# Last layer on quarters of TensorE: column product, mean and loads of x rearranged

## The chip, the cores and the metric

The program runs on one core of one Trainium2 chip. The metric is device time in microseconds (us), the median of three runs.

## The reference

Two layers on one image of 48 channels, 256 x 256, in fp32. Layer 0 is an attention over patches (group norm, a 1x1 product to q, k and v, a 3x3 depthwise convolution, attention in eight heads, a projection, the residual); the change doesn't touch it. Layer 1, cut to what matters:

```
def _L1_conv_ref(x, Ws, Hs, Cs, window_size):
    B, C, H, W = x.shape
    ws = window_size
    xb = x.reshape(B, C, H // ws, ws, W // ws, ws)
    out = jnp.einsum('bcphqw,twW,thH,tcC->bCpHqW', xb, Ws, Hs, Cs)
    return out.reshape(B, C, H, W)
...
x = x + _L1_conv_ref(_gn(x), L1_conv_Ws, L1_conv_Hs, L1_conv_Cs, 64)
```

`_gn` is a group norm with 16 groups of 3 channels. In each 64 x 64 window, and for each of three terms t, x is multiplied over its channels by Cs (48 x 48), over its columns by Ws (64 x 64) and over its rows by Hs (64 x 64); the three terms are added up.

## The kernel before, in words

The first 3230 us or so are layer 0's attention; the scheduler of the tile framework places the instructions there, and those of the next stage that are ready early slip in at its end.

**Projection and statistics (L765 to L835).** In eight steps of 16 rows from each half of the image, SyncE loads the attention's output and the input x, TensorE projects (L790), VectorE adds the residual (L797) and takes the statistics of the sum (L801), and GpSimd's queue stores the sum to a DRAM tensor `x1s` (L806). After the last step `group_stats` (L127 to L146) makes mean and reciprocal deviation: a chain of small products and VectorE instructions, with products `pm` (L132) and `pv` (L139). Then `csn`, the matrix Cs with its rows scaled by the reciprocal deviation (L828), and `cbias`, the mean times csn on all 128 partitions (L832, L834).

**Last layer (L838 to L954).** A unit is a row of windows (64 image rows, index yw) times half the width (128 columns, two windows, index xh): eight units. Each has three products:

- `over_c` (L863), the channel product: for each pair of image rows, a product of 48 channels by 128 columns with csn (144 wide: three terms by 48). The upper and lower 32 rows of the unit lie on partitions 0 to 47 and 64 to 111 of `lxq`, so two products run on two row halves of TensorE. VectorE evicts three row pairs at a time to `lzt` and subtracts cbias there (L881), eleven evictions a unit.
- `over_w` (L889), the column product: `lzt` has the 128 columns on its partitions and is the stationary operand, 64 wide; `wsb` (128 x 128 per term) is the moving one: Ws twice on the diagonal, zeros elsewhere. The two products for two groups of channels go to two column halves of TensorE. ScalarE copies each tile `pb` (128 x 512, two PSUM buffers) to `lyt` (L903).
- `over_h` (L906), the row product: `hsb` (64 x 64) stationary, `lyt` moving, 64 x 64 on each quarter of TensorE, 512 columns, three terms added up in PSUM. `residual` (L922) adds x from `lrt` on VectorE (L925), and GpSimd's queue stores to the output (L928).

The order of this stage is written out by hand (`manual_schedule`, L935): the channel product of unit 0 first; then, for every unit, three rounds (q) of eight channels from each half: two column products of four channels each from both halves (three tiles `pb` each), after each of them two groups of the next unit's channel product, and then the row product of the round before. x is loaded twice from SyncE's queue, both in packets of 512 B (128 columns): `lxq` two units ahead with the channels on the partitions (L762), `lrt` at a unit's start with image rows on the partitions (L857).

In TensorE's counts each fp32 product stands as two instructions.

Of the kernel before, what the change touches and what calls it, by code (L numbers as in the profile page):

```python
# [16 lines left out]
C = 48  # L17
# [3 lines left out]
KS = 4  # L21
# [24 lines left out]
def conv_preact_kernel(  # L46
# [80 lines left out]
    def group_stats(st, mean, rstd, pool, pspool):  # L127
# [4 lines left out]
        nc.tensor.matmul(pm, lhsT=gm, rhs=mv[:, 0:1], start=True, stop=True)  # L132
        nc.vector.tensor_copy(mean, pm)
# [5 lines left out]
        nc.tensor.matmul(pv, lhsT=gm, rhs=e, start=True, stop=True)  # L139
        f = pool.tile([P2, 1], F32, name="gsf")  # L140
# [609 lines left out]
    lx = ctx.enter_context(tc.tile_pool(name="lx", bufs=3))  # L750
    HW = WS // 2
    units = [(yw, xh) for yw in range(H // WS) for xh in range(2)]
    xqs = {}

    def load_x(u):

        yw, xh = units[u]
        xcol = slice(xh * 128, (xh + 1) * 128)
        xq = lx.tile([64 + C, HW, 128], F32, name="lxq")
        for s in range(2):  # L760
            y0 = yw * WS + s * HW
            nc.sync.dma_start(out=xq[s * 64 : s * 64 + C], in_=x1s[:, y0 : y0 + HW, xcol])  # L762
        xqs[u] = xq

    with tc.tile_pool(name="pj", bufs=3) as pj, tc.tile_pool(name="pjs", bufs=1) as pjs, tc.tile_pool(  # L765
# [41 lines left out]
        for u in range(2):  # L807
            load_x(u)

        gm2 = pjs.tile([P2, 64 + C], F32, name="gm2")  # L810
        nc.vector.memset(gm2, 0.0)
        for o in (0, 64):
            nc.vector.tensor_copy(gm2[:, o : o + C], gm[:, 0:C])
        mv1, e1 = group_stats(st1, mean1, rstd1, pjs, pp1)
        pc1 = pp1.tile([64 + C, 1], F32, name="pc1", tag="pstat")
        nc.tensor.matmul(pc1, lhsT=gm2, rhs=e1, start=True, stop=True)
        rstd2 = l1c.tile([64 + C, 1], F32, name="rstd2")
        nc.vector.tensor_scalar_add(rstd2, pc1, EPS)
        nc.scalar.activation(rstd2, rstd2, AF.Sqrt)
        nc.vector.reciprocal(rstd2, rstd2)  # L820

        csn = l1c.tile([64 + C, T3 * C], F32, name="csn")
        for s in range(2):
            nc.scalar.dma_start(
                out=csn[s * 64 : s * 64 + C].rearrange("c (t d) -> c t d", t=T3), in_=Cs.rearrange("t c d -> c t d")
            )
            r = slice(s * 64, s * 64 + C)
            nc.vector.tensor_scalar_mul(csn[r], csn[r], rstd2[r])  # L828
        mrow = pjs.tile([C, 128], F32, name="mrow")
        nc.vector.tensor_scalar_mul(mrow, ones, mean1[0:C])  # L830
        pb1 = pp1.tile([128, T3 * C], F32, name="pb1")
        nc.tensor.matmul(pb1, lhsT=mrow, rhs=csn[0:C], start=True, stop=True)  # L832
        cbias = l1c.tile([128, T3 * C], F32, name="cbias")
        nc.vector.tensor_copy(cbias, pb1)  # L834
# [3 lines left out]
    with tc.tile_pool(name="lz", bufs=2) as lz, tc.tile_pool(name="lr", bufs=2) as lr, tc.tile_pool(name="ly", bufs=4) as ly, tc.tile_pool(name="ps1", bufs=2, space=PSUM) as ps1, tc.tile_pool(  # L838
        name="ps2", bufs=2, space=PSUM
    ) as ps2, tc.tile_pool(name="ps3", bufs=1, space=PSUM) as ps3:  # L840
        wsb = lz.tile([128, T3, 128], F32, name="wsb", bufs=1)
        nc.vector.memset(wsb, 0.0)
        hsb = lz.tile([128, T3, WS], F32, name="hsb", bufs=1)
        for s in range(2):
            r = slice(s * WS, (s + 1) * WS)
            nc.scalar.dma_start(out=wsb[r, :, r], in_=Ws.rearrange("t w v -> w t v"))
            nc.scalar.dma_start(out=hsb[r], in_=Hs.rearrange("t h g -> h t g"))
        NQ = 3
        rts, zts, parts = {}, {}, {}

        def load_rows(u):

            yw, xh = units[u]
            xcol = slice(xh * 128, (xh + 1) * 128)
            rt = lr.tile([128, NQ * 8, 128], F32, name="lrt")
            for s in range(2):
                nc.sync.dma_start(  # L857
                    out=rt[s * WS : (s + 1) * WS],
                    in_=x1s[s * 24 : (s + 1) * 24, yw * WS : (yw + 1) * WS, xcol].rearrange("c y x -> y c x"),
                )  # L860
            rts[u] = rt

        def over_c(u):  # L863

            xq = xqs[u]
            zt = zts[u] = lz.tile([128, T3 * C, WS], F32, name="lzt")
            zv = zt.rearrange("p k (s y) -> p s y k", s=2)
            for y0 in range(0, HW, 3):
                n = min(3, HW - y0)
                pa = ps1.tile([128, 2, 512], F32, name="pa")  # L870
                for i in range(n):
                    for s in range(2):
                        r = slice(s * 64, s * 64 + C)
                        nc.tensor.matmul(  # L874
                            pa[:, s, i * T3 * C : (i + 1) * T3 * C],
                            lhsT=xq[r, y0 + i, :],
                            rhs=csn[r],
# [3 lines left out]
                nc.vector.tensor_tensor(  # L881
                    zv[:, :, y0 : y0 + n, :],
                    pa[:, :, : n * T3 * C].rearrange("p s (y k) -> p s y k", y=n),
                    cbias.rearrange("p (u v k) -> p u v k", u=1, v=1).to_broadcast([128, 2, n, T3 * C]),
                    ALU.subtract,
                )
                yield

        def over_w(u, c0, c1):  # L889

# [105 lines left out]
```

## Time and profile before

| what | value |
|---|---|
| median of three runs | 3678.31 us (3673.84 to 3683.65) |
| span of the profiled execution | 3669.5 us |
| TensorE busy in the span | 3466.2 us (94%) |
| VectorE, ScalarE, GpSimd busy | 2139.8, 1873.5, 542.7 us |
| first channel product starts | 3370.2 us |
| first column product starts | 3390.6 us |
| last row product ends | 3661.5 us |
| column product L896, instructions | 2304 |
| channel product L874, instructions | 1024 |
| row product L913, instructions | 576 |

The profile is of one execution. Its page gives the busy time of each engine, a map of 40 slices, the chain of work that ended last (followed back from the end, at each step to what released it), and groups of equal instructions: line, engine, operation, output and inputs, shape, count, busy time in us and mean of one in ns, then the idle time of the engine just before them and what ended it. PE is TensorE's product, PEld its load of the stationary operand, DVE VectorE, ACT ScalarE, POOL GpSimd, SP SyncE; a q after it means its queue. In lists in order of time the first two numbers are start and duration in us.

### The profile page before, as it was taken

The page shows a single profiled execution, that of the slowest core. Times are in us where ns is not written, and L with a number is a line of the kernel's source. Part 1 is how long each engine was busy: PE and PEld are TensorE (multiplying, and loading weights), DVE is VectorE, ACT ScalarE, POOL GpSimd, SP SyncE. Part 2 cuts the span into 40 slices and gives each one's busy share as a digit, 9 for nine tenths or more (in the row PEclk, how much of TensorE's full clock was granted, in tenths as well). Part 3 has the DMA queues.
Part 4 walks back from the last instruction along what each step waited for, and adds up shares of the span by engine and source line. Part 5 has one row for each costly group of instructions (what it writes and reads, how often), then busy time and mean ns, then how long its engine had stood idle before and what let it go on. Part 6 is the DMA issues. An engine that isn't in the chain of part 4 may idle for free.

```text
span 3669.5 us, 100344 instructions
## 1 busy us (share of the span) xinstructions
PE 3466.2 (94%) x44252; PEld 2907.3 (79%) x44252; DVE 2139.8 (58%) x3518; ACT 1873.5 (51%) x2747; POOL 542.7 (15%) x630
## 2 busy tenths in 40 slices
PE   2869999999999999999999999999999999965998
PEld 1337788889988888889899988888899888833776
DVE  5464674179628952895389439934993222267654
ACT  0235676566646654665466556655664444400332
POOL 2030211012211211121112112211221100010011
PEclk9989999999999999999999999999999999976999
DMA  7455665533322332333233323332333220089674
GB/s 161 154 131 147 180 171 168 158 97 92 94 72 82 98 90 80 83 93 87 78 82 92 94 76 87 86 93 71 94 84 87 65 53 19 15 213 240 116 136 93
DMA packets 275427, 386.49 MB, mean 105 GB/s; under 512 B 77330, under 2 KB 211842, under 8 KB 270952
## 3 DMA queue, kind: packets, MB, share of 16 engines
q1 hardware_dynamic: 235942, 264.95, 27.3%
q0 software_dynamic: 35552, 106.40, 12.6%
q10 hardware_dynamic: 3490, 8.64, 1.1%
q8 instruction: 350, 5.73, 0.7%
q14 instruction: 93, 0.76, 0.1%
HBM read 234.76 MB, written 144.90 MB: 103 GB/s over the span
## 4 chain that ended last, share of the span: by engine, by line
PE 84%; DVE 3%; issue 2%; DMA 2%; ACT 1%; SPq 0%; POOL 0%; ACTq 0%; POOLq 0%; DVEq 0%
PE big L337 37%; PE big L601 36%; PE pb L896 4%; PE pa L874 2%; PE pc L913 2%; DVE acc L228 1%; PE big L177 1%; PE pt L618 1%; PE pn L247 1%; DMA pot<-os__70 1%; PE pst L555 1%; DMA x1s<-pxt 0%; DMA kt<-qkv 0%; DMA t<-ot 0%; DVE ss L243 0%
## 5 line engine op out<-in xcount | busy, mean ns | idle before, releaser
L572 ACT ACTIVATE e<-big,nmx 128x1024 f32<-128x1024 f32 x1024 | 1143.9, 1117 | 878.4 <-PE big L337 617.5
L337 PE MATMUL big<-kt,qt 128*128 128x512 f32 x6144 | 1437.5, 393 | 30.2 <-DMA kt<-qkv 29.3
L601 PEld LDWEIGHTS big<-vn,e 128*64 128x64 f32 x32768 | 1358.6, 137 | 57.8 <-ACT e L572 30.6
L601 PE MATMUL big<-vn,e 128*64 128x96 f32 x32768 | 1388.9, 247 | 6.5 <-DVE oacc L612 3.0
L337 PEld LDWEIGHTS big<-kt,qt 128*128 128x128 f32 x6144 | 1146.3, 188 | 277.3 <-issue 29.2
L612 DVE TENSOR_TENSOR oacc<-big,oacc 128x768 f32<-128x768 f32 x480 | 453.5, 954 | 713.4 <-PE big L601 713.4
L228 DVE SCALAR_TENSOR_TENSOR acc<-pad,dwt,acc 126x1024 f32<-126x1024 f32 x592 | 765.6, 1293 | 39.5 <-ACT acc L209 23.7
L295 POOL DMA_DIRECT2D qkv<-o x72 | 52.7, 732 | 1242.2 <-ACT o L279 1242.2
L585 DVE TENSOR_REDUCE zt<-zs 128x1 f32<-128x4 f32 x256 | 38.5, 150 | 335.7 <-ACT e L572 335.7
L289 POOL TENSOR_TENSOR ol<-o,oh 126x1024 fp32r<-126x1024 f32 x78 | 184.6, 2367 | 311.6 <-DVE ss L243 238.9
L572 ACT ACTIVATION_READ_ACCUMULATOR e<-big,nmx 128x1 f32 x1024 | 196.4, 192 | 0.0
L903 ACT COPY lyt<-pb 128x512 f32<-128x512 f32 x144 | 84.3, 586 | 201.6 <-PE pb L896 201.6
L881 DVE TENSOR_TENSOR lzt<-pa,cbias 128x864 f32<-128x864 f32 (+1 forms) x88 | 137.0, 1628 | 85.3 <-PE pa L874 85.3
L279 ACT COPY o<-acc 126x1024 f32<-126x1024 f32 x74 | 158.6, 2143 | 0.0
L896 PEld LDWEIGHTS pb<-wsb,lzt 128*64 128x64 f32 x2304 | 125.9, 138 | 29.4 <-issue 19.7
L896 PE MATMUL pb<-wsb,lzt 128*64 128x128 f32 x2304 | 141.9, 279 | 2.8 <-issue 1.6
L623 POOL DMA_DIRECT2D os__70<-oo x128 | 64.9, 513 | 534.4 <-ACT oo L621 533.8
L790 PE MATMUL pps<-pot,wp 96*96 96x512 f32 x128 | 78.0, 777 | 55.2 <-DMA pot<-os__70 44.3
L239 ACT ACTIVATE sq<-acc 126x1024 f32<-126x1024 f32 x74 | 78.2, 1057 | 101.6 <-DVE acc L228 101.6
L180 ACT ACTIVATE ot<-big,bias 108x1024 f32<-108x1024 f32 x64 | 68.2, 1110 | 111.1 <-PE big L177 62.8
L209 ACT ACTIVATE acc<-pad,dwt 126x1024 f32<-126x1024 f32 x74 | 84.1, 1137 | 79.9 <-DMA pad<-t 79.9
L243 DVE TENSOR_REDUCE ss<-sq 126x64 f32<-126x1024 f32 x80 | 97.5, 1219 | 24.6 <-ACT sq L239 24.6
(127 smaller groups left out, 1904.8 us busy)
## 6 DMA issues: line engine op xcount, KB each, us to landing
pad<-t SPq DMA_DIRECT2D x238, 254.0 KB
t<-ot SPq DMA_DIRECT2D x128, 217.7 KB
qkv<-ol POOLq DMA_DIRECT2D x78, 336.0 KB, 6.4
qkv<-oh POOLq DMA_DIRECT2D x70, 336.0 KB, 5.6
qt<-qkv SPq DMA_DIRECT2D x176, 96.0 KB
xs<-in_x_dram SPq DMA_DIRECT2D x128, 96.0 KB
os__70<-oo POOLq DMA_DIRECT2D x128, 96.0 KB, 2.1
pot<-os__70 SPq DMA_DIRECT2D x16, 768.0 KB
```

What stands on the lines that cost most here:

```text
L209: nc.scalar.mul(self.acc, self.pad[:, 0:KS, 0:W], dwt[:, self.h, 0:1])
L228: nc.vector.scalar_tensor_tensor(self.acc, self.pad[:, dy : dy + KS, dx : dx + W], dwt[:, self.h, tap : tap + 1], self.acc, ALU.mult, ALU.add,
L243: nc.vector.tensor_reduce(self.ss, self.sq.rearrange("p a (x b) -> p x a b", b=KS), AX.XY, ALU.add)
L279: nc.scalar.copy(self.o.rearrange("p (a b) x -> p a b x", a=KS), self.acc.rearrange("p a (x b) -> p a b x", b=KS))
L289: eng.tensor_sub(self.ol, self.o, self.oh.bitcast(F32))
L337: nc.tensor.matmul(ps[:, i, :], lhsT=qt[:, r, q0 : q0 + 128], rhs=kts[2 * j + i][:, r // 2, :], start=(r == 0), stop=(r == 2),)
L572: nc.scalar.activation(e[:, j * 1024 : (j + 1) * 1024], ps.rearrange("p a b -> p (a b)"), AF.Exp, bias=nmx[:, b : b + 1], accum_out=zs[:, ...
L601: nc.tensor.matmul(ps[p : p + 64, j // 4, j % 4 * HD : (j % 4 + 1) * HD], lhsT=e[:, mb * 128 + p : mb * 128 + p + 64], rhs=vn, start=(i == 0),
L612: nc.vector.tensor_add(oaccs[h, k], ps[:, :, : 4 * HD], oaccs[h, k])
L881: nc.vector.tensor_tensor(zv[:, :, y0 : y0 + n, :], pa[:, :, : n * T3 * C].rearrange("p s (y k) -> p s y k", y=n), cbias.rearrange("p (u v ...
L896: nc.tensor.matmul(pb[s * WS : (s + 1) * WS, i, :], lhsT=zts[u][:, t * C + c + i, :], rhs=wsb[:, t, :], start=True, stop=True,)
L903: nc.scalar.copy(yt[:, t, :], pb.rearrange("p i x -> p (i x)"))
```

## The change

Seven parts, all in the last layer and just before it:

1. The column product takes quarters of TensorE. `wsb` holds Ws once per half of the partitions (128 x 3 x 64, no zeros and no memset). A tile `pb2` is now 128 x 2 x 512 for one term t and a whole round: 32 products of 64 rows by 64 columns, where the half of the partitions (w) picks the window and the PSUM bank, and s the group of channels. A round has three such tiles. There is one buffer for them; in the last unit they use the two buffers of `pa`, and VectorE copies the tile of t = 1.
2. The mean becomes a 49th row. The pieces of x are set to 1.0 at the beginning, so that row 48 (and 112) stays 1; row 48 of csn is minus the mean times csn (`mcol`, `pb1`, and a subtraction on VectorE). Evictions of the channel product are plain copies, one in four of them on ScalarE, in unit 0 one in two.
3. x is held by full image rows: five pieces of 8 row pairs of all 256 columns (`pieces`, `lx` with five tiles of 8 KB per partition instead of three of 16 KB). Unit 2n and unit 2n + 1 use the same pieces. The channel product has twelve groups a unit (3, 3 and 2 row pairs for every piece).
4. The loads after the first ones come from ScalarE's queue, one by one between its copies (`begin_load`): a piece in four loads of 48 x 4 rows, the x for the residual (`lrt`, now 8 channels by full rows, six buffers) in four loads of 64 x 4 channels for each round of a row of windows. The first pieces and the first `lrt` stay with SyncE.
5. Stores of the output go out by full rows after the second unit of a row of windows; in the last row of windows after each unit.
6. In the statistics TensorE gets products whose result nobody reads (`occupy`), seven before `pm` and one after each of `pm`, `pv`, `pc1` and `pb1`.
7. Within a round the order is: tile 0, two channel groups, tile 1, two channel groups, tile 2, the row product of the round before.

In the built change the five memsets of the pieces stand on VectorE's queue among the last four accumulations of the attention (two ahead of them, one between each two); the first waits for 18 semaphores.

```
-    def group_stats(st, mean, rstd, pool, pspool):
+    def group_stats(st, mean, rstd, pool, pspool, behind=lambda: None):
...
         nc.tensor.matmul(pm, lhsT=gm, rhs=mv[:, 0:1], start=True, stop=True)
+        behind()
...
+    pieces = [lx.tile([64 + CK, PR, W], F32, name=f"lxq{i}") for i in range(NPC + 1)]
+    for t in pieces:
+        nc.vector.memset(t, 1.0)
...
+    def load_piece(yw, i, s, y, n, eng):
+
+        y0 = yw * WS + s * HW + i * PR + y
+        eng.dma_start(out=piece(yw, i)[s * 64 : s * 64 + C, y : y + n, :], in_=x1s[:, y0 : y0 + n, :])
...
-        for u in range(2):
-            load_x(u)
...
+        for i in range(len(pieces)):
+            for s in range(2):
+                load_piece(*divmod(i, NPC), s, 0, PR, nc.sync)
...
+        busy = pps.tile([P2, KS, 128], F32, name="pps")
+
+        def occupy(n):
+
+            for _ in range(n):
+                nc.tensor.matmul(busy[:, 0:2, :], lhsT=ident[:, :P2], rhs=nmx, start=True, stop=True)
+
+        with tc.manual_schedule(engines={mybir.EngineType.PE}):
+            occupy(7)
+            mv1, e1 = group_stats(st1, mean1, rstd1, pjs, pp1, lambda: occupy(1))
...
+            nc.vector.tensor_scalar_mul(csn, csn, rstd2)
+            mcol = pjs.tile([C, 64 + CK], F32, name="mcol")
+            nc.vector.tensor_scalar_mul(mcol, at, mean1[0:C])
+            pb1 = pp1.tile([64 + CK, T3 * C], F32, name="pb1")
+            nc.tensor.matmul(pb1, lhsT=mcol, rhs=csn[0:C], start=True, stop=True)
+            occupy(1)
+            nc.vector.tensor_sub(csn, csn, pb1)
...
+        def rows_later(yw, q):
+
+            if yw < H // WS:
+                for s in range(2):
+                    for c in (0, 4):
+                        loads.append(lambda s=s, c=c: load_rows(yw, q, s, c, 4, nc.scalar))
...
+        def begin_load():
+
+            if loads:
+                loads.pop(0)()
...
+                    if (p * 3 + g) % (4 if u else 2) == 1:
+                        nc.scalar.copy(to, src)
+                    else:
+                        nc.vector.tensor_copy(to, src)
+                    if xh and g == 2:
+                        piece_later(yw * NPC + p + len(pieces))
+                    yield
...
+        def over_w(u, q, t):
+
+            end = u == NU - 1
+            pb = (ps1 if end else ps2).tile([128, 2, 512], F32, name="pb2", tag="pa" if end else "pb2")
+            for n in range(8):
+                b, i = divmod(n, 4)
+                for s in range(2):
+                    for w in range(2):
+                        r = slice(w * WS, (w + 1) * WS)
                         nc.tensor.matmul(
+                            pb[s * WS : (s + 1) * WS, w, n * WS : (n + 1) * WS],
+                            lhsT=zts[u][r, t * C + b * 24 + q * 8 + s * 4 + i, :],
+                            rhs=wsb[r, t, :],
                             start=True,
                             stop=True,
                         )
+            (nc.vector.tensor_copy if end and t == 1 else nc.scalar.copy)(
+                parts[u, q][:, t, :].rearrange("p (n w x) -> p w n x", w=2, x=WS),
+                pb.rearrange("p w (n x) -> p w n x", x=WS),
+            )
...
+                    for t in range(T3):
+                        over_w(u, q, t)
+                        begin_load()
+                        if t < 2:
+                            for _ in range(2):
+                                next(ahead, None)
+                                begin_load()
+                        elif late:
+                            over_h(*late)
```

## The prediction

> **What bounds the kernel now.** I read, in this order, the 40 slices of the page (where the last layer lies), the chain of work that ended last with its pieces in order of time, the groups by shape, and the busy time by stretch. The change touches only what runs after about 3205 us, so the chain from there on is what counts. First the start of the last layer:
>
> ```profile
> 3369.85 0.61 PE pb L832
> 3370.46 1.71 PE pa L874 x11
> 3372.19 1.64 DVE lzt L881
> 3373.88 1.83 PE pa L874 x12
> 3375.73 1.65 DVE lzt L881
> ...
> 3386.39 4.20 DVE lzt L881 x3
> 3390.63 4.75 PE pb L896 x48
> ```
>
> Until 3390.63 only the channel product of unit 0 runs. Two groups of rows take 3.55 us (3373.88 to 3377.43): TensorE is at half clock, and VectorE needs 1.65 us for each eviction, so both are late by turns. The clock is in the busy time by stretch (after PE, PEld, DVE, ACT and POOL stand the granted clock and the DMA share):
>
> ```profile
> 3370.00:3390.60 20.60, 18.09 (x130) 15.92 (x130) 17.48 (x14) 0.00 (x0) 0.00 (x0) 0.50 1.12 165
> 3395.00:3630.00 235.00, 233.41 (x3332) 179.03 (x3332) 142.69 (x96) 72.62 (x124) 26.42 (x38) 1.00 0.67 123
> ```
>
> In the second stretch TensorE is busy 233 of 235 us at full clock, VectorE 61%, ScalarE 31%. It is TensorE's own order of work that sets the end; one round (a third of a unit) and the last one, without a channel product, look like this in the chain:
>
> ```profile
> 3425.96 2.86 PE pb L896 x48
> 3428.82 1.67 PE pa L874 x24
> 3430.49 2.86 PE pb L896 x48
> 3433.35 1.67 PE pa L874 x24
> 3435.02 2.73 PE pc L913 x24
> ...
> 3649.00 5.57 PE pb L896 x96
> 3654.57 2.78 PE pc L913 x24
> ```
>
> Three rounds, 3435.02 to 3469.42, take 34.40 us: 11.47 us a round, of which the column product (L896) is 5.72, the channel product (L874) 3.0, the row product (L913) 2.74. There are 24 rounds; the last three take 5.57 + 2.74 = 8.3 us each.
>
> The groups by shape give the durations:
>
> ```profile
> L601 PE MATMUL big<-vn,e 128*64 128x96 f32 x32768 | 1388.9, 247 | 6.5 <-DVE oacc L612 3.0 <-DVE vn L591 1.9 <-ACT ot L180 1.6
> L896 PE MATMUL pb<-wsb,lzt 128*64 128x128 f32 x2304 | 141.9, 279 | 2.8 <-issue 1.6 <-DVE lzt L881 1.2
> L874 PE MATMUL pa<-csn,lxq 48*128 48x144 f32 x1024 | 84.2, 313 | 1.3 <-DVE lzt L881 1.3
> L913 PE MATMUL pc<-lyt,hsb 64*64 64x512 f32 x576 | 67.3, 598 | 1.3 <-DVE lrt L925 1.3
> L903 ACT COPY lyt<-pb 128x512 f32<-128x512 f32 x144 | 84.3, 586 | 201.6 <-PE pb L896 201.6
> ```
>
> [...] a row product of 512 columns on a quarter comes every 2.74/24 = 0.114 us though one lasts 598 ns, so four run at once. [...] the closest spacing is L601's, 10.71 us for 256 = 41.8 ns, set by its 96 columns on two halves. [...] in L896, whose products use all rows, 2.86 us for 48 leaves no room for weights (138 ns each in the PEld row) in series.
>
> **The change part by part.**
>
> *Column product on quarters.* Now 128 contraction rows meet a 128-wide matrix that is half zeros. After: no zeros, 64 rows meet 64 columns on each quarter; 192 instructions a round in place of 96 (32 products, two instructions each, for each of three tiles). Price per instruction: per column and per tile in flight the trace gives 41.8*2/96 = 0.87 ns (L601), 59.6*2/128 = 0.93 (L896), 69.6*2/144 = 0.97 (L874), 114*4/512 = 0.89 (L913). With 0.9, 64 columns on four quarters cost 64*0.9/4 = 14.4 ns; 64 instructions 0.92 us, and 0.13 for the start of a tile [...] (L874: 24 take 1.67 us and 8 take 0.69 in the chain, so 0.061 each and 0.2 for the start): 1.05 us a tile, 3.15 a round. Bounds: 0.92 (no start), [...] a wholly serial 41.8 ns is the rival below. I take 1.05 because L913 shows quarters at full rate and L601 shows 64-wide weights every 41.8 ns on two column halves, twice that many on four tiles. TensorE's round becomes 3.15 + 3.0 + 2.74 = 8.9 us.
>
> *49th row.* [...] Groups per unit go from 11 to 12, same 128 instructions: nothing on TensorE. The eviction loses its second operand. It writes with a stride, which seems what makes it slow (1675 ns for 864 elements, against 1225 ns for 1024 in the residual L925), so I keep 1.67; lower bound 864/1024*1225 = 1.03. On ScalarE between 0.87 (586 ns for 512 elements, in proportion to 0.83 ns each) and 1.8; I take 1.4.
>
> *ScalarE's round.* Three copies of 1024 elements (from 586 for 512: about 1.0, with waits 1.1 each), one eviction 1.4, and 28 loads per row of windows in six rounds, 4.7 a round. A load's issue on ScalarE's queue is not in the trace for these shapes; its weight loads held the queue 0.63 to 0.79 us, SyncE's issues of 48 long rows 0.30 to 0.42. I take 0.5, so 2.3 a round: in all 7.0 of 8.9 us. It fits, but PSUM for the column product now has a single buffer. A column tile must wait until ScalarE has copied the one before; between them lie two channel groups (1.67 us). Behind a waiting or issuing ScalarE stand exactly this copy and the next eviction, and TensorE waits for both. Walking one round through: copy 1.1, two issues 1.0, eviction 1.4, issue 0.5, then the next copy, ready at 2.7 us but begun at 4.1, so the third tile starts about 0.9 late; where fewer loads fall, not at all. I charge 0.6 a round (bounds 0 and 1.6): 9.5 us.
>
> *Loads and stores.* SyncE loses all loads after the first; nothing waited for them there. Rows of 1 KB and pieces of 4 KB replace 512 B packets; DMA was not in the chain after 3370, so nothing is gained. The first five pieces (3.9 MB in place of 3.1) follow the same last loads in the same queue. If they came late, the first channel product would start by that much later (up to 5 us); I take 0. Stores go out once per two units, 0.7 us each on GpSimd, idle there: nothing.
>
> *Five memsets* of 2048 elements fall on VectorE between the last accumulations of attention (by the 1134-element memset's 1003 ns, about 1.8 each). There VectorE is idle 1.7 us between accumulations and 4.4 us before them: 0.3 lost, up to 2 if their 18 waits are late.
>
> *Statistics.* The subtraction of the mean now precedes the first product (it needed only the scaled matrix): +0.7 us. Idle products fill TensorE's gap (3360 to 3366), one lies in a gap too short for it: +0.2. They should leave the clock full for the first unit, so its first column products cost 2.86 in place of 4.75: -1.9.
>
> *First unit.* 128 channel instructions at 0.061 = 7.8 us at full clock; evictions alternate, six on VectorE (8 to 9 us) and six on ScalarE, which first issues four weight loads (2.9 us). I take 11.5 us in place of 20.4 (3370.2 to 3390.6): -8.9. At half clock, where the timeline has 3.30 us for 24, it would be 128*0.1375 = 17.6: -2.8.
>
> **Sum.** 21 rounds * (11.47 - 9.5) = 41.4; three last rounds 8.3 to 3.15 + 2.74 = 5.9: 7.2; first unit 8.9; clock 1.9; against 0.7 + 0.2 + 0.3 = 1.2. Saved: 58.2 us. The span is 3669.5 us; the median of the three runs is 3678.3, so 8.8 lie around it and stay. 3678.3 - 58.2 = about 3620 us.
>
> **Rivals.**
> A. [...] For it: nothing in the trace is closer than 41.8 ns; against: that was the columns' price.
> B. *ScalarE becomes the bound.* Evictions at 1.8, issues at 0.7, copies late: a round of 10.5. Saved: 21*0.97 + 3*2 + 8.9 = 35: 3643. For it: the single PSUM buffer and 4.7 issues; against: 31% busy now.
> C. *Slower: the doubled instructions go singly.* If weights and products of quarters don't overlap, or TensorE's sequencer gives one pair per 41.8 ns, a tile is 2.68, a round 13.8: 21*2.3 + 3*2.5 = 56 lost, 8.9 won: 3725. It decides from about 29 to 30 ns per instruction, where 192 of them eat what the first unit saves. Against it: L913's four at once, though with one weight load per 512 columns, which proves little for 64.
>
> **Chances.** Forecast 0.52 (alone: 3604 to 3636), B 0.2, A 0.18, C 0.1. What a measurement of this kernel can tell from no change is about 0.3%, 11 us: faster 0.52 + 0.2 + 0.16 = 0.88, within 0.02 (A at its dear end), slower 0.1 (C). The range reaches from 3603 (a round of 8.9 without stalls, 12.6 less; the first unit at TensorE's 7.8, 3.7 less) to 3662 (A, and 4 of the 6 us that a half clock in the first unit would cost), which leaves out C and a little of A.
>
> **What would show it.** In the chain after: L942 with 64 instructions in about 1.05 us between channel groups; idle time of TensorE before it released by ScalarE, about 0.6 a round; seven units of some 28.5 us and a last one of 18, from about 3382 on; the clock at 1.0 from the statistics on. Wrong if a tile takes over 1.6 us (A, C), if TensorE's waits on ScalarE pass 1.5 us a round (B), or if the clock falls to half within the first unit.

## The result and the profile after

The changed kernel takes 3644.91 us (median of four runs, 3635.88 to 3654.33) against 3679.01 us for the kernel before on the same chip (four runs, 3673.84 to 3683.65): a ratio of 0.9917, 95% interval 0.9892 to 0.9942. It is faster by 34 us where 58 were forecast (3620). The profiled execution took 3654.33 us, the slowest of the four, with a span of 3652.5 us. In it layer 0 ended 8.1 us later than in the profile before (its last accumulating product, L603 after and L601 before, ends at 3232.13 against 3224.04 us), with the same code there. So the stages of the last layer are compared by themselves, from start to start:

| stage, from the two traces | before | forecast | after |
|---|---|---|---|
| `pm` (its second instruction) to the first channel product | 3.65 | 4.55 | 5.65 |
| first unit: first channel to first column product | 20.45 | 11.5 | 22.16 |
| rounds: first column product to the last row product | 270.24 | 219.7 | 241.24 |
| of these, the mean of 18 full rounds | 11.47 | 9.5 | 10.33 |
| sum of the first three rows | 294.3 | 235.8 | 269.1 |

(The forecast of the third row is 270.24 less the prediction's 41.4, 7.2 and 1.9.) The rounds won 29 us; the first unit, which was to win 8.9, lost 1.7. These stages of the two profiles account for 25.2 of the 34 us. One profile of the same work differs from the next: in the five kernels here that have these rounds and loads, this one among them, the rounds take 233.0 to 241.9 us. What is said of a stage is said of one profile.

First, the price of the quarters. A stretch of the changed kernel's chain in order of time (start and duration in us):

```profile
3435.65 0.93 PE pb L942 x64
3436.59 1.67 PE pa L916 x24
...
3441.08 1.07 PE pb L942 x58
3442.16 1.64 issue
3443.79 0.27 PE pb L942 x2
...
3452.32 0.97 PE pb L942 x54
3453.29 1.42 issue
3454.71 0.38 PE pb L942 x9
```

A column tile, 64 instructions of L942, takes 0.93 us at the top and 1.34 us without its gap in the second tile shown (1.07 + 0.27); the forecast had 1.05. But in two of these tiles TensorE stands still for 1.4 and 1.6 us in the middle, with 58 and 54 of the 64 instructions done. "issue" means that the engine waited for nothing that the profile shows. From 3433 to 3620, the 18 full rounds, the waits of TensorE are (total us, times, longest):

```profile
PE pb L942 <- issue: 9.1, 11, 1.6
PE pa L916 <- ACT lzt L926: 3.8, 4, 1.9
PE pa L916 <- issue: 2.6, 3, 1.1
PE pa L916 <- DVE lzt L928: 1.9, 5, 0.4
PE pb L942 <- ACT lyt L949: 1.5, 2, 0.8
```

The prediction charged waits for ScalarE, for the copy of a column tile and for the eviction next to it. They are 1.5 + 3.8 = 5.3 us, 0.3 a round where 0.6 was charged. "issue" is 11.7 us, 0.65 a round. All five lines are 18.9 us, 1.05 a round, so that 9.3 of the 10.33 us are left for TensorE's own work.

Five of the six waits for ScalarE stand behind a load issue that held its queue for longer than forecast, as here, where TensorE then waited 1.9 us for the eviction:

```profile
3581.86 2.78 ACTq L877
...
3584.68 1.63 ACT lzt L926
```

Second, the start. The busy time by stretch (after start, end and length: PE, PEld, DVE, ACT, POOL, granted clock, DMA share, GB/s), first unit and rounds:

```profile
3380.50:3402.70 22.20, 18.40 (x129) 15.62 (x129) 8.73 (x6) 8.73 (x6) 0.00 (x0) 0.50 0.31 57
3433.00:3619.00 186.00, 167.02 (x4661) 127.70 (x4660) 100.85 (x73) 80.37 (x72) 13.99 (x20) 0.98 0.60 143
```

The clock is at half through the whole first unit, as before. (In the trace of the changed kernel the stretches at one clock, from 3375.76 on, are 30.7 us at half, 10.2 at full, 6.8 at half, 109.2 at full; each is a multiple of 3.41 us.) The chain just ahead of it shows a gap that the idle products left:

```profile
3370.44 2.39 DVE st L807 x4
...
3372.85 1.89 DVE mv L130
...
3374.79 0.34 PE pm L132 x2
...
3376.35 1.01 PE pps L836 x2
...
3377.55 1.01 PE pps L836 x2
...
3379.39 1.11 PE pps L836 x2
...
3380.54 1.89 PE pa L916 x12
```

The seven idle products end at 3371.8; TensorE then stands idle for 3 us until `pm`, and from 3375.76 on the clock is at half. At half clock the idle products (L836) cost 1.0 to 1.1 us each, in the chain.

### The profile page after: what moved, and what is told of

It reads as the page before. It is cut to its first block, busy times and chain, and to the rows that moved or that the text cites. A ratio compares the mean times of both kernels' runs of the same rounds, so it can differ in the third digit from the quotient of the medians.

```text
span 3652.5 us, 104961 instructions
## 1 busy us (share of the span) xinstructions
PE 3426.0 (94%) x46578; PEld 2874.1 (79%) x46578; DVE 2115.9 (58%) x3505; ACT 1898.0 (52%) x2699; POOL 531.6 (15%) x616
## 4 chain that ended last, share of the span: by engine, by line
PE 81%; DMA 4%; DVE 3%; issue 2%; ACT 1%; SPq 1%; ACTq 0%; POOL 0%; POOLq 0%; DVEq 0%
PE big L339 37%; PE big L603 36%; PE pc L961 2%; PE pb L942 2%; PE pa L916 2%; PE big L179 1%; DVE acc L230 1%; PE pt L620 1%; DMA pxt<-in_x_dram 1%; DMA pad<-t 1%; PE pn L249 1%; DMA xs<-in_x_dram 1%; PE pst L557 1%; DVE xt L803 1%; DVE lzt L928 0%
## 5 line engine op out<-in xcount | busy, mean ns | idle before, releaser
L603 PEld LDWEIGHTS big<-vn,e 128*64 128x64 f32 x32768 | 1358.7, 137 | 57.1 <-ACT e L574 30.6
L603 PE MATMUL big<-vn,e 128*64 128x96 f32 x32768 | 1389.1, 247 | 5.9 <-DVE oacc L614 2.4
L928 DVE COPY lzt<-pa 128x864 f32<-128x864 f32 (+1 forms) x69 | 101.2, 1507 | 69.2 <-PE pa L916 69.2
L949 ACT COPY lyt<-pb 128x1024 f32<-128x1024 f32 x69 | 70.7, 1025 | 116.3 <-PE pb L942 96.9
L942 PEld LDWEIGHTS pb<-wsb,lzt 64*64 64x64 f32 x4608 | 82.2, 140 | 37.2 <-issue 23.4
L219 PE MATMUL dps<-pad,diag 126*126 126x512 f32 x216 | 96.3, 606 | 15.5 <-DMA pad<-t 15.5
L796 PEld LDWEIGHTS pps<-pot,wp 96*96 96x96 f32 x128 | 26.0, 212 | 107.0 <-issue 73.8
```

The source lines that it names most:

```text
L219: nc.tensor.matmul(ps[:, i, :], lhsT=diag[:, tap, :], rhs=self.pad[:, y : y + 2, dx : dx + W], start=(tap == 0), stop=(tap == 8),)
L603: nc.tensor.matmul(ps[p : p + 64, j // 4, j % 4 * HD : (j % 4 + 1) * HD], lhsT=e[:, mb * 128 + p : mb * 128 + p + 64], rhs=vn, start=(i == 0),
L796: nc.tensor.matmul(ps[:, i : i + step, :], lhsT=wp, rhs=ot[:, ki * KS + i : ki * KS + i + step, part * n : (part + 1) * n], start=True, st ...
L928: nc.vector.tensor_copy(to, src)
L942: nc.tensor.matmul(pb[s * WS : (s + 1) * WS, w, n * WS : (n + 1) * WS], lhsT=zts[u][r, t * C + b * 24 + q * 8 + s * 4 + i, :], rhs=wsb[r, ...
```

## The experiments

One theory and three rivals were to be told apart for the rounds: TensorE lacks instructions (the doubled count outruns their fetch; theory F in the recorded expectations); ScalarE's copies and load issues hold it (S); loads collide with it; the quarters themselves are worth less. For the first unit: the clock falls for the gap before `pm` (K1), for the wait behind ScalarE's load issues, or because the channel product alone keeps TensorE too little busy (K2). All kernels are edits of the changed one. Results in one table, ratios to the kernel before as measured beside each on the same chip; the stages are of each kernel's one profile, in us:

| kernel | median us | ratio, 95% interval | first unit | rounds |
|---|---|---|---|---|
| before | 3676 to 3681 | 1 | 20.45 | 270.2 |
| changed | 3644.91 | 0.9917 [0.9892, 0.9942] | 22.16 | 241.2 |
| half the instructions | 3619.48 | 0.9845 [0.9822, 0.9867] | 20.24 | 209.8 |
| loads from SyncE | 3657.49 | 0.9946 [0.9929, 0.9963] | 22.14 | 252.1 |
| 14 idle products | 3645.0 | 0.9913 [0.9891, 0.9936] | 20.20 | 236.2 |
| block diagonal | 3679.6 | 1.0001 [0.9990, 1.0013] | 21.02 | 270.5 |
| filled first unit | 3649.68 | 0.9892 [0.9850, 0.9934] | 25.93 | 233.0 |
| half tiles | 3682.59 | 1.0010 [0.9997, 1.0023] | 22.15 | 265.5 |
| no idle products | 3644.67 | 0.9897 [0.9872, 0.9922] | 22.15 | 238.1 |
| weights from SyncE | 3645.55 | 0.9913 [0.9894, 0.9933] | 19.18 | 241.9 |
| + row product spread | 3642.27 | 0.9904 [0.9886, 0.9923] | 21.23 | 232.7 |
| + six fillers | 3639.13 | 0.9886 [0.9870, 0.9903] | 15.80 | 236.3 |
| + twelve fillers | 3637.97 | 0.9897 [0.9879, 0.9915] | 17.07 | 231.3 |

**Half the instructions.** One product of 64 rows by 128 columns takes the place of two of 64 columns: the same columns stream, with half the products and half the weight loads. Left out: every second channel gets its neighbour's column product instead of its own.

```
-            for n in range(8):
+            for n in range(0, 8, 2):
-                            pb[s * WS : (s + 1) * WS, w, n * WS : (n + 1) * WS],
+                            pb[s * WS : (s + 1) * WS, w, n * WS : (n + 2) * WS],
```

> The changed kernel, but each column product is 128 columns wide (Ws stands twice side by side) and half as many are issued: every second channel gets the product of its neighbour, so the output is not the reference's; array time per tile stays at about 0.93 to 1.0 us, with 32 instructions in place of 64. Theory F (TensorE runs out of instructions: its gaps of 1 to 2 us inside a tile, each ending about 1.5 us after a 16 KB instruction packet): the gaps put down to issue inside column tiles nearly vanish, a round falls from 10.3 to about 9.7 us, total some 12 to 15 us less. Theory S (ScalarE's queue is late with copies because of its loads): a round stays within 0.2 us, since copies, evictions and loads are the same. Theory K (half clock in the first unit): the first channel product stays at 22 us.

25 us less than the changed kernel, with ScalarE's work unchanged. TensorE's waits in 19 full rounds of this kernel and one without a channel product (3414 to 3590):

```profile
PE pa L917 <- DVE lzt L929: 2.8, 6, 0.5
PE pa L917 <- ACT lzt L927: 0.4, 1, 0.4
PE pb L943 <- ACT lyt L950: 0.3, 1, 0.3
```

"issue" is gone from the list, and the waits on ScalarE fall from 5.3 to 0.7 us with it, though ScalarE now has the same work in less time. A full round is 8.94 us, 1.39 less than in the changed kernel. Not all of that is gaps: the spacings under 0.15 us within the column tiles add up to 2.46 us a round here and to 2.91 in the changed kernel, so 0.45 is paid for the instructions themselves. The other 0.9 is standing still and what follows from it. TensorE's own round on quarters, with its instructions at hand, is thus about 9.2: 8.94, less this kernel's own waits (3.5 us in 20 rounds, 0.18 each), plus 0.45. That is an estimate; it agrees with the 9.3 above.

What the gaps are can be seen in the DMA queue of instructions. From the trace of the changed kernel, its packets (16 KB each) beside TensorE's gaps; a pair is a weight load and its product, and "ready" is put at 1.5 us after the packet's end:

```
packet    took   pairs run from its start until ready   no product starts
3436.01   1.30   72                                     -
3440.76   1.42   60                                     3441.94 to 3443.79
3452.03   1.25   60                                     3453.07 to 3454.71
3455.84   0.96   71                                     -
3472.61   0.88   47                                     3473.35 to 3475.03
3491.71   1.28   57                                     3493.25 to 3494.60
```

Each gap in the table ends 1.4 to 1.6 us after such a packet has landed; the twelve gaps of over 0.4 us put down to issue from 3425 to 3619 all end 1.3 to 1.8 us after one. The page gives 368 packets for 104961 instructions, and 350 for 100344 before: 4617 more in 18 packets, about 256 in each, 128 pairs. The packets don't say for which engine they are, but the count fits TensorE alone: 368 times 256 is 94208, and the page has 46578 products and as many weight loads, 93156; before, it is 89600 against 88504. A round now has 264 pairs (168 before), so some two fetches a round, and a tile runs its 64 pairs in 0.93 us, while packet and delay take 2.4 to 2.9. In the kernel before, 22 to 50 pairs run in that time, and the whole stage has one such gap:

```profile
3406.01 1.46 PE pb L896 x22
3407.46 1.59 issue
3409.05 1.69 PE pb L896 x26
```

The doubled count alone does not make a gap. After some packets over 80 pairs run until the next are ready, without one; before the four long gaps of the table only 47 to 60 were left. What differs is the load traffic. Of the 37 fetches of the changed kernel from 3425 to 3619, 13 began when the DMA engines had been less than half busy in the 2 us before, and none of these is followed by a gap of over 0.4 us; of the other 24, 12 are. The 13 packets took 1.06 us on average, the 24 took 1.23. Counted in the same way over the nine kernels here with 64 instructions to a tile in one piece, it is 1 of 133 against 59 of 199. So in this kernel it takes both, quick instructions and a fetch that sets off among loads; the kernel of half the instructions has the loads too, and no gap. The part of the loads is read from the traces; no run takes them away.

**Loads from SyncE.** The paced loads go to SyncE's queue, where nothing holds them back but their buffers.

```
-    loads.append(lambda s=s, c=c: load_rows(yw, q, s, c, 4, nc.scalar))
+    loads.append(lambda s=s, c=c: load_rows(yw, q, s, c, 4, nc.sync))
-    loads.append(lambda s=s, y=y: load_piece(yw, i, s, y, PR // 2, nc.scalar))
+    loads.append(lambda s=s, y=y: load_piece(yw, i, s, y, PR // 2, nc.sync))
```

> The changed kernel, but the later loads of x are issued from SyncE's queue at the same places of the order, not from ScalarE's. Theory S: ScalarE's copies start on time, TensorE's idle time released by ScalarE (18 waits and 11 us at column tiles, 14 waits and 11 us at channel groups) mostly goes, a round falls from 10.3 to about 9.6 us, total some 12 to 18 us less. Theory F: only that part goes; gaps inside tiles stay at about 0.5 us a round. If the loads were the whole loss of a round, it would come to the 8.9 us of TensorE's own work. First unit unchanged at 22 us.

Slower than the changed kernel by 13 us, although ScalarE is freed of all issues. TensorE's waits from 3419 to 3635, the longest of those for issue, and a piece of its chain:

```profile
PE pb L942 <- issue: 20.7, 8, 5.6
PE pa L916 <- issue: 3.8, 3, 2.1
```

```profile
3432.91 0.38 PE pb L942 x15
3433.29 3.72 issue
3437.01 1.65 PE pb L942 x37
```

All five runs (3655.36 to 3664.10 us) are slower than the slowest of the changed kernel (3654.33), and than all of the kernel with fourteen idle products on the same chip (3643.33 to 3646.40). The waits put down to issue grow from 11.7 to 24.5 us, the longest from 1.8 to 5.6, and 30.7 us of the 18 full rounds are at half clock, against 6.8 in the changed kernel. The four longest gaps (3.3 to 5.6 us) end with a packet that began only after TensorE had run dry, and in the 4 us before each the DMA share is 1.10 to 1.14. So in this run the longest gaps lie where loads went out in bursts and the instruction packet came late; from ScalarE's queue, which lets one load go between two copies, the longest was 1.8 us. The waits for ScalarE do fall, from 5.3 to 0.3 us: its load issues cost the round what was read above, and not more. That they are not the main loss is shown by the kernel of half the instructions, which keeps them.

**Block diagonal.** Everything of the change but the quarters: the column product keeps 128 rows by 128 columns with zeros.

```
+            wsb = lz.tile([128, T3, 128], F32, name="wsb", bufs=1)
+            nc.vector.memset(wsb, 0.0)
...
+                        pb[s * WS : (s + 1) * WS, b, i * 128 : (i + 1) * 128],
+                        lhsT=zts[u][:, t * C + b * 24 + q * 8 + s * 4 + i, :],
+                        rhs=wsb[:, t, :],
```

> The changed kernel with the column product of before: 128 rows against the block diagonal matrix, two column halves, 32 instructions a tile. A tile then takes about 1.9 us in place of 1.09. If nothing but TensorE's own work set the round, it would be 5.7 + 3.0 + 2.7 = 11.4 us, and the total some 25 us more than the changed kernel's. Theories F and S: the slower tile hides both the fetch of instructions and ScalarE's queue, so that the round is within 0.2 us of 11.4 with almost no idle time of TensorE: quarters then bring 1.1 us a round of the 2.5 that their price gives, and the rest is what they uncover.

The same time as before within 0.13%, a full round of 11.58 us. A stretch of its chain:

```profile
3444.10 1.90 PE pb L941 x32
3445.99 1.43 PE pa L917 x20
```

TensorE waits for hardly anything (1.5 us from 3433 to 3620, none of it issue), and a tile costs 1.90 us where quarters take about 1.1 with the change to the next product. So six of the change's seven parts together are worth nothing measurable; the whole gain is the quarters', and three tiles at some 0.8 us less each, about 2.3 us a round, are what they offer when TensorE gets its instructions (11.58 against the 9.2 to 9.3 above).

**Half tiles.** Each column tile is cut in two, with a channel group between the halves of the first two, so that only 32 quick instructions follow each other.

```
+                        for b in range(2):
+                            over_w(u, q, t, b)
+                            begin_load()
+                            if t < 2:
                                 next(ahead, None)
```

> The changed kernel with every column tile in two halves of 32 instructions, each copied by itself, a channel group between the halves. The instructions are the same in number, but no stretch of 128 of them on TensorE takes less than about 3.9 us, where now one of 3.1 us occurs between tiles 1 and 2. Theory F: the 45 to 85 instructions at hand when a fetch begins last longer than the 2.4 to 2.9 us until it can be used, gaps inside tiles mostly vanish; [...] a round of 9.2 to 9.5 us, total 12 to 20 us less than the changed kernel. Theory S: ScalarE has six copies a round in place of three (0.59 in place of 1.01 us), its queue gets later, the round stays at 10.1 us or grows.

A miss: 3682.59 us. The gaps put down to issue do fall, to 0.6 us from 3433 to 3620, but a new wait takes their place:

```profile
PE pb L944 <- ACT lyt L951: 20.7, 29, 0.8
```

All 29 are the first product of a second half, which is in the same PSUM tile as the first and waits for ScalarE's copy of it. There the single buffer does cost what the prediction feared, because the tile is asked for twice as often.

**Fourteen idle products, and none.** `occupy(14)` instead of `occupy(7)` bridges the gap to `pm`; the other kernel leaves all idle products out.

> The changed kernel with 14 idle products ahead of the statistics in place of 7, so that TensorE has no 3 us gap before the first small product. Theory K1 (the gap alone lost the clock): full clock from the statistics on, first channel product 22 to about 11.5 us, total some 11 us less. Theory K2 (the channel product itself, with 98 of 128 rows and waits for evictions, does not hold the clock): the clock falls within the first unit, by one or a few windows of 3.4 us later than before; first channel product 15 to 21 us, total 1 to 6 us less. Rounds unchanged at 10.3 us.

> The changed kernel without idle products in the statistics. Theory K2: they bring nothing, since the clock is lost anyway before the first channel product, and at half clock they stand in the way of the small products: from the mean's product to the first channel product about 4.4 us in place of 5.65, first unit 22 us as with them, total about 1 us less. If they were of use, the first unit or the first column products would be longer without them.

With fourteen the clock is full until 3383.2, 6.6 us into the first unit (with seven it fell 4.8 us ahead of it), and then half for 17 us; the first unit takes 20.20 us, `pm` to the first channel product 4.09. Without any, 22.15 and 4.54. The totals are those of the changed kernel: as they were set, the idle products bring nothing and cost nothing that can be told. By these profiles the gap before `pm` is one cause of the half clock, not the only one.

**Filled first unit.** Fourteen, and an idle product of 128 columns after each of the first unit's twelve channel groups.

```
+            dump = ps2.tile([128, 2, 512], F32, name="pb2", tag="pb2")
             for _ in over_c(0):
-                pass
+                nc.tensor.matmul(dump[:, 0, 0:128], lhsT=ident, rhs=nmx[:, 0:128], start=True, stop=True)
```

> The changed kernel with 14 idle products ahead of the statistics and, in the first channel product, one idle product of 128 x 128 x 128 (two instructions) after each of the twelve groups. Theory K2 (the channel product's own activity is too low for the full clock): the clock stays full through the first unit, each group then costs about 0.74 us, [...] so that the first unit takes 12 to 14 us in place of 22.2, and the column products after it start at full clock; total some 9 to 12 us less. If the evictions and not the clock set the first unit, it stays at 20 us or gets longer by the idle products. Rounds unchanged at 10.1 us.

The clock still falls, at 3390.8, after this stretch of the chain:

```profile
3384.85 0.18 ACTq L866
...
3385.07 0.63 ACTq L867
...
3385.74 0.62 ACTq L866
...
3386.40 0.62 ACTq L867
...
3387.06 1.64 ACT lzt L926
```

The four weight loads (L866, L867) stand on ScalarE's queue ahead of its first eviction. From 3384.85 to 3388.74 the chain waits for it, and TensorE stands idle for 2.3 of these 3.9 us. At half clock the fillers then cost 0.72 us each.

**Weights from SyncE.** Fourteen idle products, no fillers, and those four loads moved.

```
-            nc.scalar.dma_start(out=wsb[r], in_=Ws.rearrange("t w v -> w t v"))
-            nc.scalar.dma_start(out=hsb[r], in_=Hs.rearrange("t h g -> h t g"))
+            nc.sync.dma_start(out=wsb[r], in_=Ws.rearrange("t w v -> w t v"))
+            nc.sync.dma_start(out=hsb[r], in_=Hs.rearrange("t h g -> h t g"))
```

> The changed kernel with fourteen idle products instead of seven, and with the four loads of the row and column weights (two for each half) issued from SyncE's queue instead of ScalarE's. If the half clock of the first unit comes from TensorE's wait of about 4 us for ScalarE's first channel copy, which stands behind those four issues, the clock stays full through the first unit, which falls from 22.2 us to 11 to 14 us, and the total is 8 to 10 us below the changed kernel (about 3635 to 3637). If the channel products of the first unit, at some five sixths of TensorE's time, are themselves too little for the clock, it falls one window later, the first unit takes 18 to 20 us, and the total is 2 to 4 us below. If neither the place nor the clock matters, 3645.

The second case of the three in the clock and the first unit, though not in the total, which is the changed kernel's: the clock falls at 3392.5, 5.0 us into the first unit, without the wait behind the loads. In these 5 us TensorE was busy 3.79 us.

**Row product spread.** On top of that, four of the row product's 24 instructions follow each of the first two slots' channel groups (`over_h` yields after each step).

```
+                    rows = over_h(*late) if late else iter(())
...
                         if t < 2:
                             for _ in range(2):
                                 next(ahead, None)
                                 begin_load()
+                            next(rows, None)
+                        else:
+                            for _ in rows:
+                                pass
```

> The kernel of the run before (fourteen idle products, weight loads from SyncE), with the row product of the round spread: four of its instructions after each of the first two slots' channel products, the other sixteen after the third column tile as before. If what TensorE lacks in the column tiles is instructions, fetched 256 at a time, then slower instructions laid between the quick ones give the fetch more time: fewer gaps put down to issue, and a round shorter by 0.2 to 0.4 us, 4 to 8 us in all. If the gaps fall where they fall whatever lies between the tiles, the round is the same within 0.1 us and the total within 2 us.

The trace goes the way of the first case: a full round of 9.90 us against 10.49 in the kernel without it. TensorE's waits put down to issue in the rounds:

```profile
PE pb L942 <- issue: 3.0, 4, 1.2
...
PE pc L961 <- issue: 0.7, 1, 0.7
```

3.7 us in place of 9.9 in the kernel without it. That kernel also has 17.1 us of half clock in its full rounds, and this one none, so that not all of the 0.6 us is the fetch. And the rounds vary from profile to profile: the five kernels with the row product in one piece and the changed kernel's loads have 233.0 to 241.9 us, the three with it spread 231.3 to 236.3. The medians, 3642.27 against 3645.55, are not told apart. It points to a gain of some 5 us and does not settle it.

**Fillers again, six and twelve,** on the kernel with the row product spread:

```
+            for k, _ in enumerate(over_c(0)):
+                if k % 2:
+                    nc.tensor.matmul(dump[:, 0, 0:128], lhsT=ident, rhs=nmx[:, 0:128], start=True, stop=True)
```

> The kernel of the run before (fourteen idle products, weight loads from SyncE's queue, row product spread) with an idle product of 128 columns after every second of the first unit's twelve channel groups, six in all. If the clock of the first unit falls because its channel products alone do not keep TensorE busy enough, these six keep it at full: the first unit takes 10.5 to 13 us in place of 21, and the total is 6 to 9 us below the run before (about 3634). If the six do not fill enough, or a busy TensorE is not what holds the clock there, it falls as before, the six cost about 0.7 us each at half clock, and the first unit takes 22 to 25 us.

> The same with the idle product after every one of the twelve channel groups. If busy time is what holds the clock and six are too few, the clock holds here alone: the first unit takes 12 to 15 us, since each idle product costs 0.3 to 0.4 us of TensorE at full clock. If the clock falls here too, the first unit takes 24 to 26 us, as in the run with twelve idle products and the weight loads still on ScalarE's queue, and the cause of the half clock stays open.

With six the clock holds through the whole first unit; the stretch of it by busy time:

```profile
3382.00:3397.75 15.75, 12.93 (x140) 10.24 (x140) 8.78 (x6) 8.76 (x6) 0.00 (x0) 1.00 0.40 80
```

So with these products the clock held, once the waits before it were gone: without them it fell in both kernels that have the weight loads on SyncE's queue, with them it held in both. It goes with a busier TensorE: 12.93 of 15.75 us here, against 3.79 of 5.02 in the weights kernel when it lost the clock. (The half-clock unit of the changed kernel shows 18.40 of 22.20, but its products are twice as long.) The fillers also use all 128 rows and 128 columns, where the channel product has 49 rows in each half; whether busy time or the kind of product counts is not told apart. But the unit takes 15.80 us, not 10.5 to 13, and 17.07 with twelve, not 12 to 15. The chain of the six-filler kernel says why:

```profile
3386.94 0.96 PE pa L916 x12
...
3387.92 1.64 DVE lzt L928
...
3389.60 1.03 PE pa L916 x12
...
3390.65 1.63 DVE lzt L928
```

Product and copy follow each other, in series. `pa` has two buffers, so each buffer's cycle is its product and its copy: 1.0 + 1.63 + 0.08 = 2.7 us for a group of three row pairs, 0.77 + 1.13 + 0.08 = 2.0 for one of two. Eight and four of these in two buffers are (8 * 2.7 + 4 * 2.0)/2 = 14.8, and 1.0 before the second buffer begins: 15.8. The same sum with the changed kernel's durations at half clock (1.89 and 1.36 for the products) gives 21.4, where it took 22.16. No run has another number of buffers, so this stays a sum that fits.

These two have the lowest medians of those that compute the whole reference, 3639.13 and 3637.97 us, ratios 0.9886 and 0.9897; their intervals overlap the changed kernel's. By their profiles `pm` to the last product takes 256.2 and 252.5 us against 269.1.

## Why the prediction was right in direction and 25 us too low

**Right, or nearly.** *TensorE's own round*, 8.9: 9.2 to 9.3 when the instructions are there. *The quarters' price*, 1.05 a tile: 0.93 to 1.16 in most tiles without a gap, 14.5 ns per instruction at the low end, so that four start within 58 ns. Rival A, a tile of over 1.6 us at full clock, was the author's assumption and came from no trace. *49th row*: 24 channel instructions take 1.67 us with it, as without. *Loads at nothing*: no DMA is in the chain from 3433 to 3619, and TensorE waits for none directly; but 12 of the 24 fetches that began among loads were followed by a gap, and none of the other 13, which the prediction does not have. *Evictions* with a single operand, mostly 1.61 to 1.69 us on VectorE: 1.67 was taken; on ScalarE they are near the dear end of its bracket, 1.61 to 1.72 where 1.4 was taken. (The 0.83 ns per element at its cheap end is that of ScalarE's copies in the trace before: 1012 ns for 1024 elements, L279, and 586 for 512, L903.) *Memsets*: the time from attention's last product to the first projection product is 19.5 us against 19.4.

**The step that failed: the round of 9.5.** The 0.6 us on top of 8.9 was charged to ScalarE, the single PSUM buffer and its load issues, and its upper bound was 1.6. The round measured 10.33. Of the 1.4 us on top of 8.9, 0.4 is TensorE's own work (9.3), 0.3 the charged wait for ScalarE (5.3 us in 18 rounds), 0.1 a wait for VectorE, and 0.65 the standing still that the profile calls issue. This last has no place in the prediction: the supply of instructions. The prediction counted the doubled instructions only as to TensorE's pace, in rival C, and found that four go at once; that they must also be fetched, in packets (368 of 16 KB) that the page counts on the same 16 DMA engines as the loads of x, is in none of its cases, and the "issue 1.6" in its own line of L896 was not followed up. Before, TensorE stood still in this way once in the whole stage, for 1.59 us; with four small products and their weight loads in 58 ns, and with loads under way, it did so for 11.7 us in 18 rounds. One such gap was followed by a fall of the clock as well: in the changed kernel's chain

```profile
3415.34 1.76 issue
3417.10 1.35 PE pb L942 x41
3418.45 3.18 PE pa L916 x24
3421.63 1.91 PE pb L942 x64
```

the clock is at half for 6.8 us from 3416.7 on, and 24 channel instructions take 3.18 us in place of 1.67. Not every gap is followed by one: the kernel without idle products has gaps of up to 2.5 us in its rounds, and full clock from 3405.8 to their end. In the rounds as a whole 241.2 - 219.7 = 21.5 us of the missing 33 in the profile lie here.

Rival B's time, 3643, is close to what was measured, but that is luck. Its mechanism is there only in part, 0.3 us a round: half the instructions with the same work on ScalarE made the kernel 25 us faster, and a ScalarE freed of its loads made it slower.

**The second step that failed: the first unit, 11.5.** It measured 22.16, 10.7 more. 22.16 - 15.80 = 6.4 of this is the half clock and the wait behind the weight loads together (by the six-filler kernel, which has neither), and 15.80 - 11.5 = 4.3 is an error of the sum: it let twelve evictions run on two engines side by side, 8 to 9 us, without asking how many PSUM buffers they have. With two, product and copy do not overlap within a buffer. The prediction had named the clock as what would prove it wrong, with 17.6 us; even that left the buffers out.

**Smaller terms.** A load's issue on ScalarE was put at 0.5: in the 18 rounds the middle value is 0.31 for pieces and 0.60 for rows, but 15 of the 68 took over 1 us, up to 2.78, so that the mean is 0.76. Why some are long is not shown. The statistics came to +2.0 us in place of +0.9, since the idle products within them ran at half clock. The 1.9 us for a full clock in the first column products did not come: 49 instructions took 1.98 us at 3402.70. What the run-to-run spread of layer 0 adds to the medians (the changed kernel's four runs differ by 18 us) is not explained by anything here.

## What to carry to other kernels

When an instruction is made cheaper by cutting it into more and smaller ones, count the instructions against their supply as well as against the engine: here about 256 came per fetch, by the counts above, a fetch took 2.4 to 2.9 us until it could be used (the packet's 0.9 to 1.4 in the table above and the 1.5 put after it there, an estimate), and 64 small products with their weight loads lasted 0.93 us. The page counts the instruction packets on the same 16 DMA engines as the loads (0.7% of these engines' time), so ask also what traffic they meet: here 12 of 24 fetches among loads were followed by a gap, and none of 13 others. A short "issue" in the middle of a run of equal instructions is worth a look at the instruction queue before it is laid to the nearest engine. And where product and copy follow each other in each of n PSUM buffers, as in this first unit with two, reckon with about (product + copy)/n per group, whichever engines share the copies: here (1.0 + 1.63 + 0.08)/2 = 1.4 us for three row pairs, a sum that fits the measured 15.80 us of the unit.

## What the runs showed that was not expected

- With the loads sent out unpaced the instruction gaps were longer: at most 1.8 us with the loads between ScalarE's copies, up to 5.6 us from SyncE's queue. With quiet DMA engines before the fetch there was next to no gap (1 of 133 fetches).
- A 1.8 us gap of TensorE was followed by 6.8 us of half clock, in rounds that have only two more such stretches, of 3.4 us each; in the first unit a TensorE busy about three quarters of the time lost the full clock within 5 us, and one busy 82% of the time, with six products on the full array among the others, kept it.
- The eviction of the channel product, which writes with a stride, took the same on both engines, 1.6 to 1.7 us for 864 elements (1.9 ns each; L928 on VectorE, L926 on ScalarE), while ScalarE's copy L949 of 1024 elements takes 1.01 us.
